# The sums of the next weights' squares: from a projection buffer to a bank of attention's scores, with the squares themselves spread over three row tiles

## The chip, the cores and the metric

The kernel runs on one core of a Trainium2 chip. A core has five engines with a queue of instructions each: TensorE (PE in the profile, with PEld for the loading of its weights), VectorE (DVE), ScalarE (ACT), GpSimd (POOL) and SyncE (SP), which here issues all DMA transfers. Each engine works through its own queue in order; between engines, an instruction waits for semaphores. The order of each queue is the order in which the program's calls are written. The metric is the device time of one execution in microseconds.

## The reference

The kernel computes one layer on x of 1024 x 512. It is normalised per row, then goes through two branches whose results are multiplied and added to x:

```python
xn = _layernorm(x, axis=-1)
s = _L0_attn_ref(xn, Wq, Wk, Wv, Wo, q_norm_w, k_norm_w)
g = _silu(_L0_ffn_ref(xn, gate_w, ..., down_s))
x = x + s * g
```

The attention branch has 32 query heads and 8 key/value heads of 128, four query heads to each key head:

```python
q = (x @ Wq.T).reshape(b, s, H, HD).transpose(0, 2, 1, 3)
k = (x @ Wk.T).reshape(b, s, HKV, HD).transpose(0, 2, 1, 3)
v = (x @ Wv.T).reshape(b, s, HKV, HD).transpose(0, 2, 1, 3)
q = _rmsnorm(q, q_norm_w)
k = _rmsnorm(k, k_norm_w)
scores = jnp.einsum('bkgqd,bksd->bkgqs', qg, k) / math.sqrt(HD)
attn = jax.nn.softmax(scores + bias[None], axis=-1)
out = jnp.einsum('bkgqs,bksd->bkgqd', attn, v)
return out @ Wo.T
```

The bias is causal, with a slope per head. The other branch is a gated feed-forward network with 4-bit weights that are dequantised in groups of 128. No sum of squared weights occurs in the reference: the kernel uses it to scale each head's weights to a size that fits 16-bit floats, and undoes the scale later.

## The kernel before

**Stages.** First the layer norm and the feed-forward branch run, to about 217 us of the profile. Then comes the *projection loop*, and from its last quarter on, attention. Products that need more than 16 bits are split: each operand is a high and a low 16-bit half, and `mm3` (lines 114 to 116) issues three matmuls, high by high, high by low and low by high.

**The projection loop.** There are twelve projections, numbered k: 0, 3, 6 and 9 give keys and values of two key heads ("kv"), the others queries of four heads ("q"). Iteration k of the loop (from line 1085) has eight steps t, one for each tile of 128 rows. A step works on three projections at once:

- `p.tile(row)` of projection k: twelve matmuls into one bank of PSUM (`ps`, one of two "m" buffers for even t, one of two "o" buffers for odd t). ScalarE then copies the bank to `f` (L580) and squares it head by head for the RMS norm (`jk`, L582). In a kv projection ScalarE also casts the values to 16 bits (L594), and VectorE subtracts to get their low half (L595). All of this together is called the tile's evacuation.
- `prepare(k + 1, t)`: the weights of the next projection. At t = 1 `norms` sums the squares of its weights over the partitions by a product with a matrix of ones (L518 per head, L521 for the values' columns, into `n_ps`), and VectorE makes scale factors of it (`am`, L526 and following; `al`, L536). For the last projection the same bank also takes the sums for the output weights (L524), which `wo_factors` reads (L827 to L830). At t = 2 to 5 the scaled weights are split into `wh` (ScalarE, L561 or L108) and `wl` (VectorE, L562 or L110).
- For projection k + 2: at t = 0 to 3 `load(t)` issues the DMA of a quarter of its weights (`wq` or `wkv`, L500); at t = 6 `prepare(k + 2, -1)` calls `squares`, in which ScalarE squares the loaded weights, head by head, with the sum along the row in `sa` (L507), copies the sums to 16 bits in `sb` (L510), and for kv squares the values' columns (`sq`, L512).

Each square reads all four quarters of the load. `norms` reads `sb` and `sq` one iteration after they are made.

After its tile, each step runs what had been deferred to it (`finish_step`): the inverse roots (L609, L619, L626), GpSimd's normalising (L627 to L636), and VectorE's split of the normalised rows into halves (`q` or `k`, L647 to L649). Each pair of halves is transposed by a DMA (L657) and stored by another (L662, L664), all on SyncE, and the weight loads are queued among these.

**PSUM.** There are eight banks: two score buffers "s" of two banks each (`ps2`), and two buffers each of one bank, "m" and "o" (`ps1`). Buffers of a tag are given out in turn, and a new use waits until the last reader of the old one is done. `norms` asks `spare` for its bank: for k = 0, in the feed-forward stage, a buffer of that stage, otherwise an "m" buffer. The score buffers are first used in iterations 10 and 11, where every second step also runs one step of attention (`step(early)`), which begins with `scores`. Step n of attention writes scores n and then has VectorE read scores n - 1.

Of the kernel before, what the change touches and what calls it, by code (L numbers as in the profile page):

```python
# [10 lines left out]
F32 = mybir.dt.float32  # L11
F32R = mybir.dt.float32r
F16 = mybir.dt.float16
BF16 = mybir.dt.bfloat16
# [7 lines left out]
P = 128  # L22
# [4 lines left out]
NH = 4  # L27
# [3 lines left out]
NT = S // P  # L31
HT = NT // 2
KT = DM // P
# [43 lines left out]
def attention_gated_by_ffn_kernel(ctx, tc, x, gu_w, gu_z, gu_s, dn_w, dn_z, dn_s, wq, wkv, wo, qnw, knw, out):  # L77
# [10 lines left out]
    def ps1(tag, name):  # L88
        return psum[0].tile([P, 512], F32, tag=tag, name=name)
# [59 lines left out]
    wp = left.enter_context(tc.tile_pool(name="w", bufs=1))  # L149
# [10 lines left out]
    def pair(name):  # L160
        return fpsum.tile([P, 2, 512], F32, tag="pair", name=name)
# [315 lines left out]
    def finish_step():  # L477

        for f in finishing.pop(clock[0], ()):
            f()  # L480
        clock[0] += 1
# [2 lines left out]
        finishing.setdefault(clock[0] + steps, []).append(f)  # L484

    def spare(k, name):
        return ps1("m", name) if k else pair(name)[:, 0, :]

    class Projection:
        def __init__(self, k, kind, i):  # L490
# [8 lines left out]
                self.raw = wide.tile([P, KT, 512], F32, tag="wide", name=f"w{self.name}")  # L499
            sp.dma_start(self.raw[:, j], (wq if self.kind == "q" else wkv)[self.i, :, j])  # L500

        def squares(self):
            self.sa = wp.tile([P, NH], F32, tag="sa", name=f"sa_{self.name}")
            self.sb = wp.tile([P, NH], BF16, tag="sb", name=f"sb_{self.name}")
            self.sq = wp.tile([P, KT, 256], BF16, tag="sq", name=f"sq_{self.name}")
            for i in range(self.n):
                se.activation(  # L507
                    self.sq[:, :, :HD], self.raw[:, :, i * HD : (i + 1) * HD], AF.Square, accum_out=self.sa[:, i : i + 1]
                )
            se.copy(self.sb[:, : self.n], self.sa[:, : self.n])  # L510
            if self.kind == "kv":
                se.activation(self.sq, self.raw[:, :, 256:512], AF.Square)  # L512

        def norms(self):

            n = self.n
            pn = spare(self.k, f"n2_ps{self.k}")
            te.matmul(pn[:, 256 : 256 + n], lhsT=ones_bf, rhs=self.sb[:, :n], start=True, stop=True)  # L518
            if self.kind == "kv":
                for j in range(KT):  # L520
                    te.matmul(pn[:, :256], lhsT=ones_bf, rhs=self.sq[:, j, :], start=j == 0, stop=j == KT - 1)  # L521
            wo = pn[:, 384 : 384 + HKV]
            if self.k == len(projections) - 1:
                te.matmul(wo, lhsT=ones_bf, rhs=swo16, start=True, stop=True)  # L524
            self.am = wp.tile([P, NH], F32, tag="am", name=f"am_{self.name}", bufs=2)[:, :n]
            ve.tensor_scalar(self.am, pn[:, 256 : 256 + n], 1.0 / W_SCALE**2, 1e-30, ALU.mult, ALU.max)  # L526
            rsqrt_seed(self.am, self.am)
            self.eps = eps[:, self.k, :n]
            ve.scalar_tensor_tensor(self.eps, self.am, 1e-6 * X_SCALE**2, self.am, ALU.mult, ALU.mult)
            if self.kind == "q":  # L530
                ve.tensor_tensor(self.eps, self.eps, steep, ALU.mult)
            if self.k == len(projections) - 1:
                wo_factors(wo)
            if self.kind == "kv":
                self.al = wp.tile([P, 256], F32, tag="al", name=f"al{self.i}")
                ve.tensor_scalar(self.al, pn[:, :256], DM * (X_SCALE / V_SCALE) ** 2, 1e-30, ALU.mult, ALU.max)  # L536
                rsqrt_seed(self.al, self.al)
# [128 lines left out]
    projections = []  # L666
# [4 lines left out]
    def prepare(k, t):  # L671

        if k < len(projections):
            p = projections[k]
            if t == -1:
                p.squares()
            elif t == 1:
                p.norms()
            elif t == 2:
                p.scale()  # L680
            elif t == 6:
                p.factors()
            if 2 <= t < 2 + p.n:
                p.split_head(t - 2)
            elif p.kind == "kv" and 4 <= t < 6:
                p.split_values(t - 4)
# [7 lines left out]
    for it in range(3, NI):  # L694
        if it < 3 + 2 * KT:
            projections[(it - 3) // KT].load((it - 3) % KT)
        last = it == NI - 1
        gu_unit(
            it,
            None,  # L700
            it + 1 if not last else None,
            meanwhile={NI - 2: lambda: dn_dequant(0, ve), NI - 1: down_begin}.get(it, lambda: None),
            total=not last,
        )
        if it == NI - 5:
            prepare(0, -1)
        if it == NI - 4:
            prepare(0, 1)
        if it == NI - 3:
            dn_load(0)  # L710
            dn_load(1)
        if last:
            dn_load(2)
            dn_split_h(0, 1)
# [3 lines left out]
    for it in range(NI):  # L718
        for tb in range(2):
# [17 lines left out]
            if tb:  # L737
                if 0 <= it - 3 < HKV:
                    wo_squares_load(it - 3)
                if 0 <= it - 5 < HKV:  # L740
                    wo_squares(it - 5)
                if it in (1, 2):
                    gu_total((NI - 1, None), it - 1)
                elif it == 3:
                    gu_finish(0)
                elif it == 4:
                    gu_finish(1)
                elif it == 5:
                    norm_weights()
                elif NI - 6 <= it < NI - 1:  # L750
                    prepare(0, 8 - NI + it)
                if it == NI - 2:
                    prepare(1, -1)
# [13 lines left out]
    def queue_half(p, half):  # L767

        last = p is projections[-1]

        def due(steps, i, f):
            if last and i is None:
                c = TILES + LAST_ROOTS[half]
            elif last:
                c = TILES + LAST_PAIRS[half * HT + i] - 4
            else:
                c = clock[0] + (i or 0)
            finishing.setdefault(c + steps, []).append(f)

        due(0, None, lambda: p.inverse(half))  # L780
        if p.by_root:
            due(1, None, lambda: p.newton(half, True))
        else:
            for i in range(3):
                due((i + 1) // 2, None, lambda i=i: p.newton(half, i == 0))
        for i in range(HT):
            t = half * HT + i
            due(4, i, lambda t=t: p.halves(t))
            due(2, i, lambda t=t: p.normalize(t))
# [7 lines left out]
    def load_keys(g):  # L797
        kT[g] = ap1.tile([P, NT, 2, P], F16, tag="kT", name=f"kT{g}")
        sp.dma_start(kT[g].rearrange("p t a k -> p t (a k)"), kd[g // 2][:, g % 2])

    def load_values(g):
        vT[g] = ap1.tile([P, NT, 2, HD], F16, tag="vT", name=f"vT{g}")
        sp.dma_start(vT[g].rearrange("p t a d -> p t (a d)"), vd[g])

    def load_queries(g, qb):
        qT[g, qb] = ap1.tile([P, NQT, 2, NH, P], F16, tag="qT", name=f"qT{g}_{qb}", bufs=2)
        sp.dma_start(
            qT[g, qb].rearrange("p t a g q -> p t (a g q)"), qd[g][qb * NQT : (qb + 1) * NQT].rearrange("t p c -> p t c")
        )
# [11 lines left out]
    def wo_squares_sums():  # L821
        ve.tensor_tensor(rvs, rv, rv, ALU.mult)
        ve.tensor_tensor(swo16, rvs, swo, ALU.mult)
# [168 lines left out]
    for k, (g, qbs) in enumerate(blocks[:-1]):  # L992
# [5 lines left out]
        n, taken, done = max(free, due), 0, 0  # L998
        op_first.setdefault(g, n)
        for qb in qbs:  # L1000
            for i in range(NQT):
                for part in range(NH):
# [5 lines left out]
                    if taken == 2 or n < due + done:  # L1008
                        n, taken = n + 1, 0
# [72 lines left out]
    for k, p in enumerate(projections):  # L1082
        if k == len(projections) - 3:
            load_keys(0)
            load_values(0)
            for qb in blocks[0][1]:
                load_queries(0, qb)
        for t in range(NT):
            prepare(k + 1, t)
            if t == NT - 2:  # L1090
                prepare(k + 2, -1)
            if k + 2 < len(projections) and t < KT:
                projections[k + 2].load(t)
            if t == HT:
                p.undo()
            if (k, t) == (len(projections) - 3, HT + 1):
                wo_squares_sums()

            row = t if k < len(projections) - 1 else (t + HT) % NT
            p.tile(row)  # L1100
            finish_step()
            if t % HT == HT - 1:
                queue_half(p, row // HT)
            if k >= len(projections) - 2 and t % 2 == 0:
                step(early)
                early += 1
# [46 lines left out]
```

## Time and profile before

| what | value |
|---|---|
| time, median of 3 runs | 1066.62 us (1066.06 to 1070.48) |
| the profiled execution's own time | 1066.42 us |
| its span | 1064.6 us |
| TensorE busy | 1002.7 us, 94% of the span |
| VectorE busy | 886.1 us, 83% |
| ScalarE busy | 802.7 us, 75% |
| GpSimd busy | 413.9 us, 39% |
| projection loop alone (217 to 433 us: iterations 0 to 9) | about 21.6 us for one iteration |
| iterations 10 and 11, with eight steps of attention | 433 to 496 us |

Times in the profile are microseconds from the start of the span. In a row of the timeline there are the start, the duration, the engine, the line of the kernel, the operation, what it writes and reads, and in brackets the idle time of the engine before it with what ended that. L114 to L116 are the lines of `mm3`, whatever product calls it, so these rows are told apart by their tiles (`ps_q`, `s`, `av`). Matmuls overlap in the pipeline, so a row of 0.38 us can start 0.22 us after the last. A wait for several events is put down to the one that came last by the profile.

### The profile page before, as it was taken

Reading aid. Unit: us, or ns where it says so; the run is one execution under the profiler, and the core shown is the slowest. Engines: PE = TensorE matmul, PEld = TensorE weight load, DVE = VectorE, ACT = ScalarE, POOL = GpSimd, SP = SyncE. Lnnn points to the kernel's source line nnn. Section 1 sums busy time; section 2 is a strip of 40 time slices with the busy share of each in tenths; the row PEclk is TensorE's granted clock in tenths of the full one; section 3 lists DMA queues with packets and bytes.
Section 4 is the critical chain, followed back from the end, with each engine's and each line's share of the span. In section 5 each row is a group of like instructions: output and inputs, shape, how many; then the busy total and the mean of one; then the engine's idle time right before and its main releaser. Section 6 shows DMA issues by size and latency. Waiting matters only on the chain.

```text
span 1064.6 us, 18405 instructions
## 1 busy us (share of the span) xinstructions
PE 1002.7 (94%) x5913; PEld 584.6 (55%) x5913; DVE 886.1 (83%) x1745; ACT 802.7 (75%) x2160; POOL 413.9 (39%) x407
## 2 busy tenths in 40 slices
PE   7899899999989999898799999999999999999986
PEld 4344377844444444344566666566666666665563
DVE  7888996638778687788799899898998998979986
ACT  5777644778877787587778788797987888868862
POOL 2588653124545546361343215123141141250732
PEclk9999999999999999999999999999999999999998
DMA  6123259447988989989999999899999998999995
GB/s 202 49 100 119 70 170 302 166 139 162 219 228 188 242 203 235 279 179 207 226 193 214 195 200 222 167 227 197 189 207 193 197 223 182 221 224 194 231 189 129
DMA packets 455039, 204.39 MB, mean 192 GB/s; under 512 B 401506, under 2 KB 411038, under 8 KB 454942
## 3 DMA queue, kind: packets, MB, share of 16 engines
q1 hardware_dynamic: 454942, 203.21, 85.4%
q8 instruction: 46, 0.75, 0.3%
q14 instruction: 51, 0.42, 0.1%
HBM read 77.32 MB, written 27.27 MB: 98 GB/s over the span
## 4 chain that ended last, share of the span: by engine, by line
PE 48%; DVE 17%; ACT 13%; issue 10%; DMA 8%; SPq 2%; POOL 2%; DVEq 0%; ACTq 0%; POOLq 0%
PE gu_ps L267 6%; DMA pT<-p 4%; PE s L114 4%; DVE pf L878 3%; PE s L116 3%; PE s L115 3%; PE op L114 3%; PE op L115 3%; PE av L114 3%; PE op L116 3%; PE av L116 3%; PE av L115 3%; ACT p L898 2%; ACT pf L879 2%; PE ps_q L114 2%
## 5 line engine op out<-in xcount | busy, mean ns | idle before, releaser
L907 DVE SCALAR_TENSOR_TENSOR p<-pf,row,p 128x1024 f16<-128x1024 f32 (+7 forms) x256 | 227.8, 890 | 23.5 <-ACT p L898 20.3
L879 ACT ACTIVATE pf<-pf,row 128x1024 f32<-128x1024 f32 (+7 forms) x256 | 197.6, 772 | 57.2 <-DVE row L878 52.7
L878 DVE CUSTOM_DVE_ANT_0 pf<-s,trel,cs 128x1024 f32<-128x1024 f32 (+7 forms) x256 | 207.2, 809 | 13.7 <-PE s L116 13.4
L898 ACT ACTIVATE p<-pf,row 128x1024 f16<-128x1024 f32 (+7 forms) x256 | 196.5, 768 | 8.4 <-DMA pT<-p 3.5
L114 PE MATMUL av<-pT,vT 128*128 128x256 f16 (+1 forms) x640 | 167.8, 262 | 15.5 <-DMA pT<-p 15.5
L115 PE MATMUL av<-pT,vT 128*128 128x256 f16 (+1 forms) x640 | 167.8, 262 | 0.0
L116 PE MATMUL av<-pT,vT 128*128 128x256 f16 (+1 forms) x640 | 167.6, 262 | 0.0
L114 PE MATMUL s<-kT,qT 128*128 128x512 f16 (+3 forms) x384 | 125.0, 325 | 12.4 <-DVE row L878 12.1
L115 PE MATMUL s<-kT,qT 128*128 128x512 f16 (+3 forms) x384 | 125.0, 326 | 0.0
L116 PE MATMUL s<-kT,qT 128*128 128x512 f16 (+3 forms) x384 | 123.4, 326 | 0.0
L837 POOL TENSOR_SCALAR wor<-wor,rvs 128x512 f32<-128x512 f32 x32 | 54.5, 1702 | 162.8 <-DMA wor<-in_wo 141.5
L114 PE MATMUL ps_q<-wh_q,xth 128*128 128x512 f16 x256 | 97.6, 381 | 2.6 <-DVE am_q L526 2.5
L116 PE MATMUL ps_q<-wh_q,xtl 128*128 128x512 f16 x256 | 97.5, 381 | 0.0
L115 PE MATMUL ps_q<-wl_q,xth 128*128 128x512 f16 x256 | 97.5, 381 | 0.0
L114 PE MATMUL op<-woh,oh 128*128 128x512 f16 x248 | 94.5, 381 | 0.0
L115 PE MATMUL op<-wol,oh 128*128 128x512 f16 x248 | 94.3, 380 | 0.0
L116 PE MATMUL op<-woh,ol 128*128 128x512 f16 x248 | 94.2, 380 | 0.0
L114 PEld LDWEIGHTS <-vT 128*128 128x128 f16 x640 | 62.6, 98 | 56.6 <-DMA pT<-p 9.4
L115 PEld LDWEIGHTS <-vT 128*128 128x128 f16 x640 | 62.6, 98 | 41.3 <-issue 3.5
L941 ACT ACTIVATE oh<-av 128x256 f16<-128x256 f32 x128 | 47.7, 373 | 48.5 <-PE av L116 47.8
L636 POOL TENSOR_TENSOR f_q<-f_q,inv_q 128x512 f32<-128x512 f32 x64 | 77.4, 1237 | 1.1
L844 POOL TENSOR_TENSOR wol<-wor,woh 128x512 f16<-128x512 f32 x32 | 49.4, 1543 | 71.3 <-ACT woh L843 71.3
(194 smaller groups left out, 2255.6 us busy)
## 6 DMA issues: line engine op xcount, KB each, us to landing
qd<-tr_q SPq DMA_DIRECT2D x56, 256.0 KB, 3.4
qT<-qd SPq DMA_DIRECT2D x28, 512.0 KB, 4.5
wq<-in_wq SPq DMA_DIRECT2D x32, 256.0 KB, 3.9
wo_sq<-in_wo SPq DMA_DIRECT2D x8, 1024.0 KB, 9.1
wor<-in_wo SPq DMA_DIRECT2D x32, 256.0 KB, 3.7
gui<-in_gu_w SPq DMA_DIRECT2D x13, 512.0 KB, 3.5
wkv<-in_wkv SPq DMA_DIRECT2D x16, 256.0 KB, 3.8
vd<-v SPq DMA_DIRECT2D x8, 512.0 KB, 4.0
```

The lines of the kernel that those rows point to most:

```text
L114: te.matmul(ps, lhsT=lh, rhs=rh, start=first, stop=False)
L115: te.matmul(ps, lhsT=lh, rhs=rl, start=False, stop=False)
L116: te.matmul(ps, lhsT=ll, rhs=rh, start=False, stop=last)
L267: te.matmul(banks[j][:, k, :], lhsT=w[:, j, ws], rhs=x[:, j, k * 512 : k * 512 + 512], start=x is xth, stop=x is xtl)
L636: ge.tensor_tensor(f, f, ib, ALU.mult)
L837: ge.tensor_scalar(wor[g, i], wor[g, i], rvs[:, g : g + 1], None, ALU.mult)
L844: ge.tensor_tensor(wol[g, i], raw, woh[g, i], ALU.subtract)
L878: ve.tensor_tensor_reduce(p, ps, trel[g][:, S - w :], cs[:, hh : hh + 1], 3e38, ALU.add, ALU.min, least[:, c])
L879: se.activation(p, p, AF.Exp, bias=least[:, c], scale=-1.0, accum_out=total[:, c])
L898: se.activation(p16[u, qt][:, :, 0, :], pf[u, qt], AF.Copy, scale=scale[:, qt : qt + 1])
L907: ve.scalar_tensor_tensor(lo, p, scale, hi, ALU.mult, ALU.subtract)
L941: se.activation(oh, av_ps[u], AF.Copy, scale=1.0 / P_SCALE)
```

## The change

`spare` gives `norms` the first bank of a score buffer in place of an "m" buffer for k > 0. `squares` takes an index: indices below n are the squares of one head each, index n is the copy to `sb` and, for kv, the square of the values' columns. In the loop these are called at t = 5, 6 and 7 instead of all at t = 6: for a q projection (n = 4) indices 0 and 1, then 2, then 3 and 4; for a kv projection (n = 2) index 0, then 1, then 2. For the last projection, `norms` is called at t = 0 instead of t = 1, ahead of the first scores. In the feed-forward stage the squares of projections 0 and 1 stay together.

```diff
     def spare(k, name):
-        return ps1("m", name) if k else pair(name)[:, 0, :]
+        return (ps2 if k else pair)(name)[:, 0, :]
...
-        def squares(self):
-            self.sa = wp.tile([P, NH], F32, tag="sa", name=f"sa_{self.name}")
...
-            for i in range(self.n):
+        def squares(self, i):
+            if i == 0:
+                self.sa = wp.tile([P, NH], F32, tag="sa", name=f"sa_{self.name}")
...
+            if i < self.n:
                 se.activation(
                     self.sq[:, :, :HD], self.raw[:, :, i * HD : (i + 1) * HD], AF.Square, accum_out=self.sa[:, i : i + 1]
                 )
+                return
             se.copy(self.sb[:, : self.n], self.sa[:, : self.n])
             if self.kind == "kv":
                 se.activation(self.sq, self.raw[:, :, 256:512], AF.Square)
...
             if t == -1:
-                p.squares()
-            elif t == 1:
+                for i in range(p.n + 1):
+                    p.squares(i)
+            elif t == (0 if k == len(projections) - 1 else 1):
                 p.norms()
...
         for t in range(NT):
             prepare(k + 1, t)
-            if t == NT - 2:
-                prepare(k + 2, -1)
-            if k + 2 < len(projections) and t < KT:
-                projections[k + 2].load(t)
+            if k + 2 < len(projections):
+                if t < KT:
+                    projections[k + 2].load(t)
+                n = projections[k + 2].n
+                for i in (range(n + 1)[: n // 2], range(n + 1)[n // 2 : n - n // 4], range(n + 1)[n - n // 4 :])[t - 5] if t >= 5 else ():
+                    projections[k + 2].squares(i)
```

More of the change, by code (lines that the diff above doesn't have):

```diff
@@ L500, in load @@
             sp.dma_start(self.raw[:, j], (wq if self.kind == "q" else wkv)[self.i, :, j])
-        def squares(self):
-            self.sa = wp.tile([P, NH], F32, tag="sa", name=f"sa_{self.name}")
-            self.sb = wp.tile([P, NH], BF16, tag="sb", name=f"sb_{self.name}")
-            self.sq = wp.tile([P, KT, 256], BF16, tag="sq", name=f"sq_{self.name}")
-            for i in range(self.n):
+        def squares(self, i):
+            if i == 0:
+                self.sa = wp.tile([P, NH], F32, tag="sa", name=f"sa_{self.name}")
+                self.sb = wp.tile([P, NH], BF16, tag="sb", name=f"sb_{self.name}")
+                self.sq = wp.tile([P, KT, 256], BF16, tag="sq", name=f"sq_{self.name}")
+            if i < self.n:
                 se.activation(
```

## The prediction

> **What bounds the kernel now.** I read the totals first, then TensorE's waits in the stage that the edit touches (the projection loop, 217 to 496 us), then each wait in order of time, then the chain of work that ended last. [...] TensorE is busy 94% of the span. Its waits from 223 to 500 us are:
>
> ```profile
> PE n_ps L518 <- DVE v L595: 5.6, 3, 2.7
> PE s L114 <- DVE row L878: 4.4, 4, 1.8
> PE ps_q L114 <- DVE am_q L526: 2.5, 2, 1.2
> PE n_ps L518 <- ACT jk_q L582: 0.3, 1, 0.3
> ```
>
> Columns: total us, times, longest. Rows one, three and four are the "m" bank: the squares' product (L518) takes one of two "m" buffers, so it waits until row tile 6 of the iteration before is evacuated, and row tile 2 waits until VectorE has read the product. That is 8.4 us, all that the new bank can remove. In the order of time:
>
> ```profile
> 305.03 0.17 PE L518 MATMUL n_ps<-sb_q,ones_bf 128*128 128x4 bf16 x1 [1.46 <-DVE v L595]
> 309.05 0.38 PE L114 MATMUL ps_q<-wh_q,xth 128*128 128x512 f16 x1 [1.24 <-DVE am_q L526]
> ...
> 327.60 0.16 PE L518 MATMUL n_ps<-sb_kv,ones_bf 128*128 128x2 bf16 x1 [0.26 <-ACT jk_q L582]
> ...
> 440.07 0.16 PE L518 MATMUL n_ps<-sb_q,ones_bf 128*128 128x4 bf16 x1 [2.71 <-DVE v L595]
> 440.12 0.59 PE L114 MATMUL ps_q<-wh_q,xth 128*128 128x512 f16 x1
> ```
>
> The number in brackets is TensorE's idle time. The first two (iteration 4) recur in iteration 7 at 371.71 and 375.72. A row tile is 12 matmuls started 0.2157 us apart, 2.59 us. After the idle time at 440 the tile took from 440.12 to 444.03, 3.9 us: its matmuls lasted 0.63 us instead of 0.38, at a granted clock of 0.83 over 434 to 444 us. So that one wait cost 2.7 + 1.3 us.
>
> But the waits are not the bound on their own. ScalarE also waits, for the weights that it squares:
>
> ```profile
> 323.37 0.63 ACT L507 ACTIVATE sq_kv<-wkv 128x512 bf16<-128x512 f32 x1 [2.14 <-DMA wkv<-in_wkv]
> 389.25 0.63 ACT L507 ACTIVATE sq_kv<-wkv 128x512 bf16<-128x512 f32 x1 [1.34 <-DMA wkv<-in_wkv]
> 435.29 0.63 ACT L507 ACTIVATE sq_q<-wq 128x512 bf16<-128x512 f32 x1 [2.29 <-DMA wq<-in_wq]
> ```
>
> and the chain that ended last runs through exactly that:
>
> ```profile
> 317.79 5.50 DMA wkv<-in_wkv
> ...
> 324.88 0.19 ACT sb_kv L510
> 325.07 0.96 ACT sq_kv L512
> 326.03 0.47 ACT f_q L580
> 326.50 1.05 ACT jk_q L582 x8
> 327.56 0.04 issue
> 327.60 0.16 PE n_ps L518
> ```
>
> The fourth load lands, the squares follow, a tile's evacuation, then TensorE. The DMA engines are 0.87 busy over 223 to 440 us, and SyncE issues the loads in order among transposes that wait for VectorE. So the squares of iterations 4, 7 and 9 can't begin earlier.
>
> **The change, part by part.** *The bank.* Eleven products (projections 1 to 11) leave "m". Removed where TensorE pays now: in iterations 4 and 7 the wait of row tile 2 (gap 1.62 less the normal 0.22: 1.4 us each), and part of the product's own wait. No operation is added; the score buffers are unused until iteration 10.
>
> *The squares.* Seven projections of queries have four squares and a copy, 3.1 us of ScalarE (277.44 to 280.57); three of keys and values have two, a copy and a 1024-wide square, 2.6 us (323.37 to 325.94). All stood ahead of tile 6's evacuation. Now they stand ahead of tiles 5, 6 and 7: two squares, then one, then one and the copy (for keys and values one, one, then the copy and the wide square). Neither DMAs nor SyncE's order move, since the four loads are issued at t = 0 to 3 as before; ScalarE's sum is unchanged. Two things follow. The copy that the product reads now stands behind tile 6's evacuation: 1.03 us later for keys and values, 1.48 for queries (325.94 to 327.42), about the moment when the old "m" wait ended. And the first square comes one evacuation earlier, so it meets a load that hasn't landed; queued behind the waiting square are the evacuations of tiles 5, 6 and 7, and behind these the copy, TensorE's product and VectorE's subtraction L595.
>
> *Iterations 3 to 4 and 6 to 7* (load in time). Copy done at about 304.5 instead of 303.4; TensorE arrives at 303.4 and goes on at 304.5, not 305.03. With tile 2's wait gone it is 0.5 + 1.4 = 2.0 us ahead. ScalarE and VectorE gain only 0.8: at 307.83 ScalarE's evacuation starts as VectorE's last q subtraction (307.03, 0.69) frees its f buffer, whatever the profile names. They go 0.8 earlier because tile 6 is no longer behind the whole burst.
>
> *Iterations 4 to 5 and 7 to 8* (load late). ScalarE waits from tile 5 on. I let the load land 0.8 us earlier with VectorE: 322.5 instead of 323.3. From there 0.75 (square) + 1.48 (tile 5) + 0.75 + 1.48 (tile 6) + 1.1 (copy and wide square) = 5.6: product at 328.1, now 327.60, +0.5. Likewise 388.4 + 5.6 = 394.0, now 393.85: +0.2. From both sides, each lies between -1 (a load 2 us earlier) and +1.3 (no earlier load). TensorE, 2 us ahead, then stands idle 2.9 and 2.2 us. [...] By the row at 440, a gap of 2.8 us costs a tile at the slower clock, 1.3 us; the gaps of 1.62 at 309 and 375 cost none. [...]
>
> *Iterations 5 and 8* (load just in time). The loads land at 338.99 + 4.0 = 343.0 and 405.93 + 3.4 = 409.3; the first square now would start at 342.6 and 408.6. ScalarE loses 0.4 and 0.7: +1.1, inside a stretch where it never rests (408 to 417) and VectorE waits 4.7 us for it.
>
> *Iteration 9 to 10.* Projection 11's product moves from t = 1 to t = 0, with its five VectorE operations on am and eps and the five of wo_factors (444.82 to 446.8, 2.0 us). TensorE now has row tile 0 (2.59) and scores 0 (1.19) queued behind it; VectorE has two half tiles of keys, which have slack, since SyncE's transposes for them come last. The load lands at 435.25 as now (issued 430.19, 5.1 us). Then two squares 1.5, tile 5 1.03, square 0.75, tile 6 1.03, square and copy 0.85: 440.4. TensorE arrives at 433.47 and stands 7 us. Then product, tile 0 with 1.3 us of slow clock, scores 0, tile 1: ends at 448.1; now 444.03. +4.1 on TensorE. What follows has slack: ScalarE idles 0.58 at 447.05 and 1.78 at 451.76, so its first exponential, and VectorE's row behind it, come about 2.2 later. From 440 to 485 TensorE never rests (44.9 of 45 us), but from 485 to 525 it stands 10.4 us behind VectorE's rows and pT's transposes, so only the 2.2 reach the end. Bounds: 0 (all absorbed) to 4.1. Scores 1 now takes the product's slot: VectorE reads it by about 446, TensorE wants it after tile 2 (450): nothing, and up to 2 us if VectorE is later.
>
> **Sum:** 0.7 + 2.0 + 1.1 + 2.2 = 6.0, less 0.3 for a stall at 222.50 (0.15) and others at 348 and 417: +5.7. The removed waits are in these terms already. The profiled execution took 1066.42 us (span 1064.6 and 1.8 around it), 0.2 under the median of 1066.62; so 1072.2.
>
> **Rivals.** *The wait is absorbed:* TensorE's shift is eaten in 485 to 525 and the clock holds. For it: 10.4 us of idle time there, and DMA at 1.04, a bound of its own. Against: VectorE's rows there descend from the late exponentials. 1067.5. *Faster:* the loads come early. If SyncE's fourth loads land 3 us sooner because VectorE, freed of the burst, feeds its transposes sooner, every product finds its copy ready: 3.0 in each of iterations 4 and 7 are saved, in 9 about 2.7 + 1.3, less part given back: 1060. Against: VectorE waited only 2.6 us at tile 6, of which I find 0.8 usable. It decides at about 2 us earlier. *Much slower:* in iteration 9 the subtraction of tile 5 (now 433.03) waits until 437.8 behind the stalled ScalarE, the transposes and value stores behind it collide with the start of attention, where DMA is full, and the 4.1 and more come through: 1080. Against: VectorE now idles from 434.6 to 439.6 anyway.
>
> **How the numbers follow.** Forecast 0.50 (own range 1069 to 1077), absorbed 0.24, faster 0.16, much slower 0.10. Half a per cent, about what a measurement of this kernel can tell from no change, is 5.3 us: 1061.3 to 1071.9. Slower: 0.36 of the forecast's and the 0.10; same: 0.14, 0.24 and 0.01; faster 0.15. The range, 1061 to 1079, leaves out about a tenth at each end.
>
> **What would show it.** Right: the waits of L518 on L595 and of row tiles on L526 gone; L518 waiting for sb's copy (L510), most at iteration 10, 5 us or more; the squares' waits for wkv and wq longer than 5.8 us; slow matmuls after 440. Wrong: those loads issued 2 us or more earlier, L518 without waits, or TensorE's idle time from 485 to 525 down by as much as the stage before grew.

## The result and the profile after

Over 20 runs each, the changed kernel takes 1068.05 us (1064.94 to 1072.22) and the kernel before 1068.68 us (1066.06 to 1071.97). The ratio is 0.9999, with a 95% interval of 0.9988 to 1.001: no difference. Runs of one kernel differ by 6 to 7 us, and much of that arises late in attention: in two profiles of the changed kernel the last exponential came 825.6 and 822.5 us after the first evacuation of iteration 0, in the opposite order to the earlier marks. Over these 20 runs a longer time goes with a lower mean granted clock (correlation -0.74). So below I read marks inside the trace beside the totals.

TensorE's waits from 223 to 500 us with the change (total us, times, longest; L520 and L523 are the former L518 and L521):

```profile
PE n_ps L520 <- ACT sb_q L512: 7.5, 3, 6.0
PE s L114 <- DVE row L881: 2.6, 2, 1.8
PE n_ps L520 <- ACT sb_kv L512: 2.4, 2, 1.4
PE n_ps L523 <- ACT sq_kv L514: 1.6, 2, 0.8
```

Both waits for the "m" bank are gone. In their place the product waits for the squares and for their copy, 11.5 us instead of the 8.4 that were removed. The timeline shows where:

```profile
303.75 0.16 PE L520 MATMUL n_ps<-sb_q,ones_bf 128*128 128x4 bf16 x1 [0.50 <-ACT sb_q L512]
...
325.69 0.16 PE L520 MATMUL n_ps<-sb_kv,ones_bf 128*128 128x2 bf16 x1 [1.04 <-ACT sb_kv L512]
326.65 0.60 PE L523 MATMUL n_ps<-sq_kv,ones_bf 128*128 128x256 bf16 x4 [0.79 <-ACT sq_kv L514]
...
369.69 0.16 PE L520 MATMUL n_ps<-sb_q,ones_bf 128*128 128x4 bf16 x1 [0.98 <-ACT sb_q L512]
...
438.38 0.16 PE L520 MATMUL n_ps<-sb_q,ones_bf 128*128 128x4 bf16 x1 [5.99 <-ACT sb_q L512]
438.41 0.17 PE L526 MATMUL n_ps<-swo,ones_bf 128*128 128x8 bf16 x1
438.44 0.59 PE L114 MATMUL ps_q<-wh_q,xth 128*128 128x512 f16 x1
438.82 0.63 PE L115 MATMUL ps_q<-wl_q,xth 128*128 128x512 f16 x1
```

Most of it is one wait, at iteration 10, and row tile 0 behind it runs at the slow clock (granted clock 0.50 until 442.45 us): its successor starts at 442.99, so it took 4.55 us instead of 2.59. Busy time by stage shows the same; the columns are the stage, TensorE, its weight loads, VectorE, ScalarE, GpSimd, granted clock, DMA share and GB/s. Before:

```profile
434.00:444.00 10.00, 7.29 (x31) 3.04 (x30) 4.90 (x13) 6.63 (x30) 3.15 (x8) 0.83 1.10 285
485.00:525.00 40.00, 29.61 (x214) 19.64 (x213) 30.55 (x57) 33.30 (x85) 11.69 (x8) 1.00 1.04 215
```

and with the change:

```profile
434.00:444.00 10.00, 5.62 (x20) 2.24 (x20) 7.29 (x22) 6.09 (x30) 4.26 (x8) 0.66 1.08 266
485.00:525.00 40.00, 32.88 (x222) 21.09 (x220) 31.26 (x57) 33.56 (x85) 11.44 (x8) 0.96 1.08 225
```

TensorE does less in the ten microseconds at iteration 10. From 485 to 525 it runs eight matmuls more than before, where it used to stand idle, but the 3.3 us of added busy time are not all work made up: the granted clock is 0.96 there, half from 514.13 to 517.54 us, and at half clock matmuls take longer (0.63 us instead of 0.38, as at 438.82).

ScalarE's squares that wait for weights, with the change, and the copy that TensorE waits for:

```profile
321.20 0.63 ACT L508 ACTIVATE sq_kv<-wkv 128x512 bf16<-128x512 f32 x1 [2.35 <-DMA wkv<-in_wkv]
387.47 0.63 ACT L508 ACTIVATE sq_kv<-wkv 128x512 bf16<-128x512 f32 x1 [2.70 <-DMA wkv<-in_wkv]
433.29 0.63 ACT L508 ACTIVATE sq_q<-wq 128x512 bf16<-128x512 f32 x1 [2.32 <-DMA wq<-in_wq]
...
438.14 0.19 ACT L512 CAST sb_q<-sa_q 128x4 bf16<-128x4 f32 x1
```

They start 2.2, 1.8 and 2.0 us earlier than before (323.37, 389.25, 435.29): the loads landed sooner than I had allowed. But from the last of these to the copy it is 4.85 us, where before it was 3.01 (435.29 to 438.30). The load's 2.0 us are all but spent.

To follow this through the runs, the table has marks read from ScalarE's timeline in one profile of each kernel, in us from the first evacuation of iteration 0: the first evacuations of iterations 7, 9 and 10, the last projection's first square and copy, and the 11th and 46th exponential of attention. "Ratio" is the time against the kernel before.

| kernel | it. 7 | it. 9 | first square | copy | it. 10 | 11th exp | 46th exp | ratio (95%) |
|---|---|---|---|---|---|---|---|---|
| before | 153.68 | 195.37 | 214.46 | 217.47 | 221.75 | 280.60 | 356.21 | |
| before, again | 153.69 | 195.18 | 214.40 | 217.42 | 221.70 | 280.54 | 356.51 | |
| the change | 152.21 | 194.42 | 212.45 | 217.30 | 222.39 | 280.92 | 357.14 | 0.9999 (0.9988 to 1.001) |
| the change, again | 153.23 | 195.49 | 213.22 | 218.06 | 223.19 | 281.70 | 358.06 | |
| last product in "m", t = 1 | 151.70 | 195.48 | 213.72 | 218.57 | 222.19 | 281.45 | 357.45 | 1.0003 (0.999 to 1.0015) |
| bank only | 152.51 | 194.89 | 214.44 | 217.45 | 222.91 | 281.58 | 358.40 | 1.0016 (1.0005 to 1.0027) |
| spread only | 152.69 | 196.06 | 211.68 | 216.51 | 220.13 | 279.39 | 355.13 | 1.0008 (0.9996 to 1.002) |
| early loads | 151.06 | 191.77 | 207.69 | 212.53 | 218.19 | 276.76 | 354.12 | 0.9989 (0.9977 to 1.0) |
| early loads, last in "m" | 151.18 | 191.87 | 208.35 | 213.19 | 216.79 | 275.62 | 353.65 | 0.998 (0.9969 to 0.9992) |
| early loads and squares | 148.28 | 188.69 | 204.87 | 212.15 | 217.81 | 277.43 | 353.56 | 0.9989 (0.9973 to 1.0005) |
| all loads early | 148.12 | 188.10 | 197.56 | 211.79 | 217.06 | 276.44 | 353.44 | 0.9936 (0.9911 to 0.9962) |
| all loads early, last in "m" | 147.88 | 187.47 | 196.19 | 208.72 | 213.66 | 273.21 | 349.78 | 0.9953 (0.9928 to 0.9977) |
| last squares together | 151.78 | 194.76 | 212.42 | 215.44 | 221.46 | 280.33 | 357.17 | 1.0 (0.9986 to 1.0015) |
| the same, last in "m" | 152.06 | 195.17 | 211.07 | 214.09 | 220.11 | 279.52 | 355.81 | 0.9997 (0.9986 to 1.0009) |

### The profile page after: what moved, and what is told of

The parts are those of the page before. It is cut to its first block, busy times and chain, and to the rows that moved or that the text cites. A ratio compares the mean times of both kernels' runs of the same rounds, so it can differ in the third digit from the quotient of the medians.

```text
span 1069.1 us, 18405 instructions
## 1 busy us (share of the span) xinstructions
PE 1004.0 (94%) x5913; PEld 585.5 (55%) x5913; DVE 888.2 (83%) x1745; ACT 799.8 (75%) x2160; POOL 416.8 (39%) x407
## 4 chain that ended last, share of the span: by engine, by line
PE 54%; DVE 16%; issue 10%; ACT 10%; DMA 7%; POOL 3%; SPq 0%; DVEq 0%; ACTq 0%; POOLq 0%
PE gu_ps L267 6%; PE s L114 4%; PE s L116 4%; PE s L115 4%; DMA pT<-p 4%; PE av L114 4%; PE op L115 3%; PE op L114 3%; PE op L116 3%; PE av L116 3%; PE av L115 3%; DVE pf L881 3%; PE ps_q L114 3%; PE ps_q L115 3%; PE ps_q L116 3%
```

## The experiments

Three theories stood at the start. A: the change gains in iterations 3 to 9, and gives it back because the last projection's product was moved ahead of row tile 0 and waits there. B: the start of attention has a bound of its own and absorbs any shift. C: the bank gains and the spreading adds nothing; A, by contrast, says that the spreading alone brings the gain. All kernels compute the whole layer.

**How far the marks carry.** Both kernels, unchanged, were profiled once more.

> The kernel before, unchanged, profiled once more, to see how far the marks in the trace vary by themselves. If they are to carry differences of half a microsecond, the time from the first evacuation of iteration 0 to that of iteration 7 (153.68 us) and to the eleventh exponential (280.60 us) repeats within 0.3 us; if transfers land by chance, within 1 us or more, and the change's 0.3 us there says nothing.

> The changed kernel, unchanged, profiled once more: from the first evacuation to iteration 7's 152.21 us and to the eleventh exponential 280.92 us in the first profile. Under the explanation by the last product: again 1 us or more under the kernel before at iteration 7, a wait of about 6 us of the product at iteration 10, and no gain left at the eleventh exponential.

The kernel before repeats within 0.2 us up to iteration 10 and 0.06 at the 11th exponential. The changed kernel does not: 1.0 us at iteration 7, 1.1 at iteration 9, 0.8 at the 11th exponential; the wait at iteration 10 is 5.69 us. So a gain of 0.5 to 1.5 us at iteration 7 and none left at the 11th exponential (0.3 and 1.1 us later than before) holds in both profiles, and single differences under 1 us don't count.

Three runs further down (the last product in "m", the last squares together, and both) differ from the change from row tile 5 of iteration 9 on at the earliest, so up to iteration 9's mark they are three more profiles of it. In the five, iteration 4's mark lies at 86.23 to 86.28 (87.00 in both profiles of the kernel before), iteration 7's at 151.70 to 153.23 and iteration 9's at 194.42 to 195.49. On average the change is 0.7, 1.5 and 0.3 us ahead: most of its lead is gone before the last product comes up.

Much of the scatter is the clock. These are stretches of the second profile of the change, then of the first, around the product in iteration 4 (columns as above):

```profile
325.50:328.91 3.41, 1.42 (x9) 0.76 (x8) 2.62 (x3) 3.41 (x16) 3.41 (x3) 1.00 0.60 133
328.91:332.32 3.41, 3.41 (x10) 1.22 (x9) 2.12 (x10) 2.67 (x19) 0.14 (x1) 0.50 0.59 149
...
322.98:326.39 3.41, 1.84 (x9) 0.78 (x8) 3.38 (x3) 3.41 (x17) 3.41 (x4) 1.00 0.54 127
326.39:329.80 3.41, 3.15 (x17) 1.66 (x17) 1.54 (x9) 3.35 (x20) 0.95 (x1) 1.00 0.54 119
```

In the second profile TensorE's idle time of 1.20 and 0.79 us there is followed by 3.41 us at half clock, and iteration 5 takes ScalarE 21.91 us, from its first evacuation to the next iteration's. In the other four profiles it takes 21.09 to 21.11. Two of the three later runs have such a stretch around the start of iteration 8, which then takes 21.91 and 21.93 us instead of 21.08 or 21.09. The last section sets such stretches beside the idle time ahead of them.

**Each half alone.** First the bank without the spreading, then the spreading without the bank:

```diff
-                for i in (range(n + 1)[: n // 2], range(n + 1)[n // 2 : n - n // 4], range(n + 1)[n - n // 4 :])[t - 5] if t >= 5 else ():
+                for i in range(n + 1) if t == 6 else ():
```

> The bank moves to a score buffer (last product at t = 0), but the squares stay together at t = 6. Theory A: the spreading alone brings ScalarE and VectorE forward, so here iteration 7's tile 0 is evacuated at about 374.2, hardly earlier than before (374.51); TensorE waits at L518's place for the copy, about 1 us or less in iterations 4 to 8, and 4 to 5 us at iteration 10; eleventh exponential at 502 to 503. Theory C (the removed wait for the bank is what gains, spreading adds nothing): iteration 7 as in the changed kernel, 373.1.

```diff
-        return (ps2 if k else pair)(name)[:, 0, :]
+        return ps1("m", name) if k else pair(name)[:, 0, :]
...
-            elif t == (0 if k == len(projections) - 1 else 1):
+            elif t == 1:
```

> The squares are spread over t = 5, 6, 7, but the product stays in an m buffer at t = 1. Theory A: ScalarE and VectorE still come about 0.7 us forward in each of iterations 4 and 7 (tile 0 of iteration 7 evacuated at about 373.2), since their order is what sets the pace there; TensorE keeps the waits for the m buffer; eleventh exponential at about 500. Theory C: no gain, iteration 7 at 374.5 and eleventh exponential at 501.4 or later.

Each alone is about 1 us ahead at iteration 7 (152.51 and 152.69 against 153.68), which is within the 1.5 us by which the change itself varies there. Iteration 4's mark is steadier: 86.64 with the bank alone and 86.53 with the spreading alone, against 87.00 before and about 86.26 with both. By this each half gains something, 0.4 and 0.5 us, so neither theory holds as written. I had expected hardly anything of the bank there. From iteration 9 they part. With the bank and the last product ahead of row tile 0, iteration 10's mark comes 28.0 us after iteration 9's, as with the whole change (28.0 and 27.7). Before it is 26.4; with the spreading alone, where the last product stays at t = 1, 24.1. TensorE's timeline at iteration 10, bank only:

```profile
440.38 0.16 PE L520 MATMUL n_ps<-sb_q,ones_bf 128*128 128x4 bf16 x1 [7.31 <-ACT sb_q L512]
```

and its waits from 223 to 500 us, spread only:

```profile
PE s L114 <- DVE row L881: 4.7, 4, 1.8
PE ps_q L114 <- DVE am_q L528: 4.4, 2, 2.2
PE ps_q L114 <- ACT jk_q L584: 1.8, 1, 1.8
PE n_ps L520 <- ACT sb_q L512: 1.2, 2, 0.7
```

In the second the "m" buffer's wait stands (L528: 2.2 us at row tile 2 in two iterations, longer than before), but there is no long wait at iteration 10. Part of the 24.1 is chance: in that run the load came in time. In the total, bank only is 0.16% slower; spread only can't be told from before, although its 11th exponential is 1.2 us earlier.

**The last product alone put back.** Ten products in score buffers, the eleventh in "m" at t = 1:

```diff
     def spare(k, name):
+        if k == len(projections) - 1:
+            return ps1("m", name)
         return (ps2 if k else pair)(name)[:, 0, :]
...
-            elif t == (0 if k == len(projections) - 1 else 1):
+            elif t == 1:
```

> The change, except that the last projection's product stays in an m buffer at t = 1, as before. Theory A (the gain of iterations 3 to 9 is given back because the last product was moved ahead of row tile 0 and scores 0 and waits there for squares behind a late load): iteration 7 starts as in the changed kernel (tile 0's evacuation near 373.1 us, before 374.5); TensorE's wait at iteration 10 falls from 6.0 to about 2.4 us, and the eleventh exponential of attention, at 501.43 before and 501.76 with the change, comes at 499.5 to 500. Median about 1.5 us under the kernel before. Theory B (the start of attention has a bound of its own, the DMA engines, and absorbs any shift): eleventh exponential at 501.2 to 501.8 whatever TensorE's wait is, and the same time.

TensorE's wait fell to 2.0 us as expected, but the 11th exponential came at 281.45, not under 280. Theory A fails here: the place of the last product is not the whole loss. Its copy was itself late, 218.57 against 217.47 before. From the copy to iteration 10's first evacuation it is 3.6 us with the product at t = 1, and 5.1 with it at t = 0 (222.39 - 217.30; 223.19 - 218.06): there, row tile 0 and its slow clock come after the copy instead of before it. Against the second profile of the change, which begins iteration 9 at the same moment (195.49), iteration 10 comes 1.0 us earlier and the 11th exponential 0.25. The product's place costs about 1 us at iteration 10; the late copy costs as well.

**The copy brought forward.** The last projection's squares all before row tile 5, so that no evacuation stands between them; then the same with the last product in "m":

```diff
-                for i in (range(n + 1)[: n // 2], ...)[t - 5] if t >= 5 else ():
+                parts = (range(n + 1), (), ()) if k + 2 == len(projections) - 1 else (range(n + 1)[: n // 2], ...)
+                for i in parts[t - 5] if t >= 5 else ():
```

> The changed kernel, but the last projection's four squares and the copy all stand ahead of row tile 5 of iteration 9 (t = 5), with no evacuation between them; the other projections stay spread. Theory D, formed from the runs so far: the eleventh exponential comes 63 to 64 us after the last projection's copy is done, and the spreading puts two evacuations (2 x 0.9 us) between that load and the copy. Then the copy comes 3.1 us after the first square instead of 4.9, and the eleventh exponential, from the first evacuation, at 279 to 280 (280.92 and 281.70 in the two profiles of the change). If instead something else sets that stage's pace, it stays at 281 or later. By the scatter of where the load lands, either can be off by 1 us; the distance from first square to copy can't.

> As the run beside it, and the last product in an m buffer at t = 1 (only the other ten in score buffers). Theory D with a cost of 0.5 to 1 us for putting the product ahead of row tile 0: eleventh exponential at 278.5 to 279, some 62.5 to 63 us after the copy. If the place of the product costs nothing: as in the run beside it.

The timeline of ScalarE in the first of the two:

```profile
434.95 0.63 ACT L508 ACTIVATE sq_q<-wq 128x512 bf16<-128x512 f32 x1 [1.95 <-DMA wq<-in_wq]
...
437.97 0.19 ACT L512 CAST sb_q<-sa_q 128x4 bf16<-128x4 f32 x1
```

From first square to copy it is 3.02 us instead of 4.85, and the 11th exponential comes at 280.33, 0.6 and 1.4 us before the two profiles of the change, just outside the 279 to 280 expected. With both undone it is 279.52, 1.4 and 2.2 us before them and 1.1 us before the kernel before. So the two things done to the last projection probably cost about 1 us together. More is not shown: the 0.6 is under what counts, and part of this run's 1.4 to 2.2 is chance, since its load came in time and ScalarE waited only 0.15 us for it. But theory D fails as a rule: the 11th exponential is not 63 us behind the copy (64.9 and 65.4 here). Once the copy is early, the evacuations of row tiles 5 to 7, now behind the squares, may set the pace; this I did not test. Both totals are those of the kernel before.

**The late load.** Loads two row tiles earlier, the first half in the iteration before:

```diff
-                if t < KT:
-                    projections[k + 2].load(t)
+                if k == 0 and t < 2:
+                    projections[2].load(2 * t)
+                    projections[2].load(2 * t + 1)
+                elif k and t < 2:
+                    projections[k + 2].load(2 + t)
+                if t >= 6 and k + 3 < len(projections):
+                    projections[k + 3].load(t - 6)
```

> The change, with each weight load issued two row tiles earlier (the first half at t = 6 and 7 of the iteration before). Theory A: ScalarE's waits for wkv and wq (7.3 us with the change) go to under 1 us; the last product waits 3 us instead of 6.0 on TensorE; eleventh exponential near 499.5 to 500. Theory B: eleventh exponential unchanged at 501.2 to 501.8, since the DMA engines have the same work. A third possibility: the loads, put ahead of transposes on SyncE, delay those, and VectorE comes later by 1 us or more.

ScalarE's waits for weights vanish, and the 11th exponential comes 3.8 us earlier than before, more than expected. So the late loads were what held this stretch back. Of the 3.8, 2.1 are left at the 46th exponential, and the ratio is 0.9989. With the last product in "m" as well:

> Early loads, and the last projection's product in an m buffer at t = 1. With early loads alone TensorE still stands 4.0 us at iteration 10 and then runs a tile at the slow clock; here row tile 0 and scores 0 come first, so the wait falls to under 1 us. Theory A (TensorE's wait at iteration 10 is paid in full by the end, because TensorE never rests from 525 to 577 us): the 46th exponential, 577.04 before and 575.10 with early loads alone, comes at 572 to 573, and the median is near 1063.5. Theory B (the start of attention absorbs it): 46th exponential at 575, median 1066.

TensorE's wait for the copy at iteration 10 falls from 4.0 to 0.5 us, but row tile 2 now waits 2.2 for the "m" buffer; 1.1 us are gained at the 11th exponential, 0.5 at the 46th. That is nearer to theory B, which had the 46th exponential at 575 in the profile's own time (it came at 575.07). Then early loads with the squares a row tile earlier, at t = 4, 5, 6 (`[t - 4] if 4 <= t < 7`), last product at t = 0:

> Early loads, the product in a score buffer, last one at t = 0, and the squares at t = 4, 5, 6 instead of 5, 6, 7, so that the copy is done one row tile before TensorE asks for it. Theory A: no wait of the product on the copy anywhere (under 1 us in all; 7.0 with early loads alone), no slow clock at iteration 10; 46th exponential at 571.5 to 573, median near 1063. Theory B: 46th exponential at 575, median 1066.

Theory A fails: the product waits 7.3 us at iteration 10. Iteration 9 starts 6.7 us earlier than before, and by the 11th exponential over half of that is lost again (3.2 us are left). The first line is ScalarE's in iteration 9, from its timeline:

```profile
426.19 0.63 ACT L508 ACTIVATE sq_q<-wq 128x512 bf16<-128x512 f32 x1 [7.43 <-DMA wq<-in_wq]
```

and TensorE's at iteration 10:

```profile
433.72 0.16 PE L520 MATMUL n_ps<-sb_q,ones_bf 128*128 128x4 bf16 x1 [7.26 <-ACT sb_q L512]
```

Half of the last load is issued at 415.83 and 421.11, on SyncE behind attention's first keys, values and queries, 1.5 MB issued from 414.25 to 415.35. So in the last pair all four quarters are issued at t = 6 and 7:

```diff
-                elif k and t < 2:
-                    projections[k + 2].load(2 + t)
                 if t >= 6 and k + 3 < len(projections):
-                    projections[k + 3].load(t - 6)
+                    projections[k + 3].load(2 * t - 12)
+                    projections[k + 3].load(2 * t - 11)
```

> All four quarters of a weight load are issued at t = 6 and 7 of the iteration before (so projection 11's come ahead of attention's first keys, values and queries on SyncE, behind which two of them stood in the run with early squares, where ScalarE waited 7.4 us in iteration 9), squares at t = 4, 5, 6, product in a score buffer, last one at t = 0. Theory A: the product's wait at iteration 10, 7.3 us there, falls under 1 us and the slow clock goes with it; marks from the first evacuation: iteration 9 at 188.5 to 189, iteration 10 at 210 to 212 (217.81), eleventh exponential 270 to 272 (277.43), 46th 350 to 352 (353.56); median near 1063 to 1064, 0.3% under the kernel before. Theory B (from 485 us on the DMA engines or TensorE's own work set the pace and absorb what is gained): eleventh exponential at 270 to 272, but 46th still near 353, median 1065.5.

> As the run beside it, but the last projection's product in an m buffer at t = 1. With its weights early, the place of the last product should not matter: Theory A has the same marks within 0.5 us as with the product at t = 0; if the m buffer itself costs, row tile 2 of iteration 10 waits up to 2 us for tile 0's evacuation, as in the run with early loads and the m buffer, and the marks are 1 to 2 us later.

These two are faster than the kernel before, by more than the interval: ratios of 0.9936 and 0.9953, medians 1062.38 and 1063.3 us. Early loads and squares were not run without the bank and the spreading, so what they would give alone is open. The marks expected from iteration 10 on were wrong: in the first of the two the load is in time, yet the product waits 6.9 us at iteration 10, and the place of the last product does matter. ScalarE's waits from 418 to 436 us name the next bound:

```profile
ACT inv_kv L621 <- DVE ms_kv L611: 6.2, 1, 6.2
ACT f_kv L582 <- DVE q L651: 2.2, 1, 2.2
ACT sq_q L508 <- DMA wq<-in_wq: 0.5, 1, 0.5
```

and VectorE's timeline at the same place:

```profile
429.50 0.43 DVE L650 CAST q<-f_q 128x512 f16<-128x512 f32 x1 [4.20 <-DMA tr_q<-q]
```

VectorE waits for a transpose to land before it can reuse its buffer of halves; ScalarE waits for VectorE, and the rest of the spread squares wait on ScalarE. With the last product at t = 1 TensorE has row tile 0 and scores 0 to do meanwhile and the product does not wait at all; the marks are 3.2 us earlier at the 11th exponential and 3.7 at the 46th. The totals of the two, six and eight runs, don't tell them apart.

## Why the prediction was right and wrong

The measured time lies inside the range of 1061 to 1079, and the outcome "same" had been given 0.39. The likeliest case, 1072.2 us with its own range of 1069 to 1077, was wrong: the width of the range and the weight of the rivals made the number right, not the mechanism. The outcome has the time of the rival "absorbed", but only in part its mechanism: in its first profile a gain and a loss of about 1 us cancel inside the projection loop.

*The bank: right.* The waits on L595 and L526 are gone, and the product's wait for the copy took their place. The forecast had the product at 304.5 us in iteration 4; it was 303.75. ScalarE's first evacuation there was to come 0.8 us earlier and came 0.7 to 0.8 earlier in all five profiles.

*Iterations 4 to 5 and 7 to 8: the sign was wrong.* The step that failed is "I let the load land 0.8 us earlier with VectorE". The first squares start 2.2 and 1.8 us earlier. In iteration 4 the last load was issued only 0.2 us earlier (317.62, before 317.79): it landed within about 3.5 us instead of 5.5. I had kept the old transfer time. Why it was shorter is open. In iteration 7 it was issued 1.6 us earlier (383.07, before 384.70), about as much as the loop was ahead by then. The 5.6 us from load to product were right (321.20 to 326.65, 5.45), so the product came at 325.7 to 326.7 and not at 328.1. ScalarE keeps less of this: from the first square to the next iteration's first evacuation it is 6.7 us in both places, where it was 5.5, since row tile 5's evacuation now stands behind the square too. So its lead of 1.5 us at iteration 7 is 0.6 at iteration 8 (173.34 against 173.94 us from the first evacuation).

*The slow clock: a chance, taken as nearly sure.* In the first profile TensorE stood 1.04 + 0.79 and 1.37 + 0.79 us in these two places, not 2.9 and 2.2, and no matmul was slow after. No run shows the 2.0 us that the sum has for this; it was my estimate, and in the first profile it was nothing. Over the five profiles half clock followed in one in the first place and in two in the second, after gaps of 1.2 to 2.1 us and then 0.79 us, and cost TensorE 1.3 to 1.7 us each time. At iteration 10 a gap of 6.0 us cost 2.0 us, where 1.3 was taken.

*Iterations 5 and 8: nothing, not 1.1.* In the first profile the last loads were issued at 337.15 and 403.15 instead of 338.99 and 405.93, and the squares found them there.

*Iteration 9 to 10: right mechanism, half the size.* Copy 4.85 us after the first square, wait of 6.0 where 7 was forecast. TensorE arrived 1.25 us earlier than before and ended row tile 1 2.7 us later: 3.9 us lost, 4.1 forecast. What came through to the 11th exponential, counted from iteration 9, is 1.3 us in one profile and 1.0 in the other (86.50 and 86.21 against 85.23), where 2.2 was taken.

Together: 1 us ahead or level at iteration 9, where the sum had 3.8 us behind, and 1.0 to 1.3 given back, where it had 2.2. The rival "faster" set its turning point at loads 2 us earlier. They came about that much earlier, and nothing was won, since ScalarE's new order spent it between load and copy. The runs with early loads show that the rival's idea, that the load decides, was sound in part: with the loads in time the 11th exponential comes 3.8 us earlier, but with all of them early the product at t = 0 still waits 6.9 us.

## What to carry to other kernels

Before a wait for a buffer is removed, follow what feeds the instruction that waits: here the product's input was a copy behind squares behind a late load, and issuing that load and its squares earlier on top of the bank and the spreading, gave 0.5 to 0.6% where these alone gave nothing. Spreading a burst lets its neighbours through sooner but makes its last part later by all that is put between (here 4.85 us from first square to copy, instead of 3.01); spread only what nobody waits for. A step moved up to suit a buffer's turn takes its inputs' deadline with it.

## What was not expected of the hardware

From its issue to the square that waited for it, the last 256 KB of iteration 4's weight load took 5.6 us in both profiles of the kernel before, and 3.6 to 4.5 us in the five of the change, at nearly the same moment of the loop. Why is open.

The granted clock was at half for stretches of a few microseconds: in the kernel before from 439.41 to 442.82 us (3.41 us), from within a gap of 2.71; in the change from 435.62 to 442.45 (6.83 us), from within the gap of 5.99, and from 514.13 to 517.54 (3.41 us), from 0.8 us after a gap of 2.95. After shorter gaps it went both ways. TensorE's timeline at the start of iteration 8 with the last squares together, then with the last product in "m" as well:

```profile
394.00 0.16 PE L520 MATMUL n_ps<-sb_kv,ones_bf 128*128 128x2 bf16 x1 [2.15 <-ACT sb_kv L512]
394.95 0.60 PE L523 MATMUL n_ps<-sq_kv,ones_bf 128*128 128x256 bf16 x4 [0.80 <-ACT sq_kv L514]
395.39 0.38 PE L114 MATMUL ps_q<-wh_q,xth 128*128 128x512 f16 x1
...
392.09 0.16 PE L522 MATMUL n_ps<-sb_kv,ones_bf 128*128 128x2 bf16 x1 [1.44 <-ACT sb_kv L514]
393.04 0.91 PE L525 MATMUL n_ps<-sq_kv,ones_bf 128*128 128x256 bf16 x4 [0.79 <-ACT sq_kv L516]
393.74 0.63 PE L114 MATMUL ps_q<-wh_q,xth 128*128 128x512 f16 x1
```

Behind gaps of 2.15 and 0.80 us the next row tile's matmuls took 0.38 us, behind the shorter 1.44 and 0.79 they took 0.63. So the length of a gap alone does not tell whether a slow stretch follows; what does is left open. TensorE can stand idle for part of such a stretch: of the 6.83 us at iteration 10, 2.76 lay in the gap, and it cost 2.0 us; the stretch of 3.41 us in the kernel before cost 1.3 us.
